# Two samples' counts stacked in one matmul and evicted as 16-bit integers

## The chip, the cores and the metric

The kernel runs on one core of a Trainium2 chip. A core has five engines that run side by side, each with its own instruction order: TensorE (matmuls; PE in the profile, and PEld for its weight loads), VectorE (DVE), ScalarE (ACT), GpSimd (POOL) and SyncE (SP, which here only issues DMAs). [...] The metric is device time in microseconds.

## The reference

A recommender's forward pass for 16384 samples: a mean of 32 word vectors of 300 floats, three means over 20 vectors of 64, four single vectors of 64, a "wide" sum of one float per lookup, and a small MLP.

```python
tok = word_emb[token_idx].mean(axis=1)               # 32 of 50000 rows, 300 wide
e1 = emb_mh1[mh1_idx].mean(axis=1)                   # 20 of 1000 rows, 64 wide
e2, e3 = ...                                         # 20 of 5000, 20 of 10000
o1, o2, o3, o4 = ...                                 # one row each of 100, 50, 20, 1000
emb = jnp.concatenate([tok, e1, e2, e3, o1, o2, o3, o4], axis=1)   # 748
wide = (the same lookups in tables of width 1, summed)[:, None]
h = jax.nn.relu(emb @ W1 + b1)                       # 1024
h = jax.nn.relu(h @ W2 + b2)                         # 512
h = jax.nn.relu(h @ W3 + b3)                         # 256
return jax.nn.sigmoid(h @ Wd + bd + wide)
```

## The kernel before, in words

The samples go through in 128 tiles of 128. Work is emitted in steps by one loop written out by hand (lines 570 to 620): 11 steps per tile (`STEPS`), 1408 steps with counts and 16 more to finish (`WAKE`), 1424 in all. Each engine executes its instructions in the order in which that loop emits them.

**Word vectors.** Each of the 128 x 32 sets of 128 rows is fetched by one indirect DMA that GpSimd issues (`tokens`, L255), two to a buffer, eight buffers (`TOK_BUFS`). `add_up` (L237 to L243) adds them into a PSUM accumulator on VectorE, three groups later (`TOK_LAG`). The loop hands out these gathers evenly over the 1424 steps.

**Small tables.** The seven small tables are not gathered. They lie on the chip as `terms`: 138 slices (`n_h`) of 128 rows, each row as three bf16 parts which together keep float precision (`convert_tables`). For each sample the kernel counts how often each table row is looked up, and multiplies the counts with the tables:

- `one_hots` (L322, VectorE) compares keys with an iota. For six samples of each half tile (`ONEHOT`; four in the last step of a tile) it makes `row1`, where lookup p hits row r of a slice, and `slice1`, where it hits slice h. A partition is one lookup: 64 lookups of a sample on partitions 0 to 63, 64 of another sample on 64 to 127. The one-hots for step i + 1 are emitted ahead of the counts of step i, in two buffers.
- `counts` (L340, TensorE) multiplies them: rows x slices, 128 x 138 counts for each sample. Each matmul uses 64 partitions, one sample's lookups; 12 in a full step.
- The eviction (L347, ScalarE) copies the 12 results out of PSUM as fp8 into `cnt`, ordered half, sample, slice.
- `small_sums` (L365, TensorE), for the tile before, takes for each slice the counts of its 128 samples as weights (`by_slice[:, :, h]`, elements 138 bytes apart) and `terms[:, h, :]` as the moving operand, and sums in PSUM over slices; VectorE adds the three parts up (L371).

**MLP.** Two tiles form a block. `Block.add_small` and `add_tokens` transpose the sums; `layer` (L461, TensorE, float32) makes the products, with a ReLU on ScalarE (L470) after each row of outputs, in two PSUM buffers `ph`. The loop spreads a block's layers over the steps (`Paced`). `early_part` (L443) begins the last block's first layer in the PSUM buffers of the counts.

Count results have one buffer `pc` of four PSUM banks. Indices are loaded by SyncE, `ix` for four tiles at a time (L276), and the keys brought into columns by a transpose (`key_columns`, L305).

Of the kernel before, what the change touches and what calls it, by code (L numbers as in the profile page):

```python
# [11 lines left out]
I32 = mybir.dt.int32  # L12
U32 = mybir.dt.uint32
AF = mybir.ActivationFunctionType
ALU = mybir.AluOpType
AX = mybir.AxisListType

P = 128
# [10 lines left out]
LAYER_TILES = 2  # L29
HALF = P // 2  # L30
N_SMALL = 3 * N_MH + 4
ONEHOT = 6
# [19 lines left out]
def kernel(  # L52
# [94 lines left out]
    terms = const.tile([P, n_h, 3 * ROW], BF16, name="terms")  # L147
    minus_half = const.tile([P, P], BF16, name="minus_half")
    nc.vector.tensor_single_scalar(minus_half, ident, -0.5, op=ALU.mult)

# [16 lines left out]
    def convert_tables():  # L167
# [19 lines left out]
        def make(p, c):  # L187

            if c == 0:
                nc.scalar.activation(term(p, 0), rows(p), AF.Copy, scale=2.0)  # L190
                return
            _, a, b = pieces[p]
            left = ps_h.tile([P, SPLIT, ROW], F32, name="left", tag="ph")[:, 0 : b - a, :]
            nc.tensor.matmul(left, ident, rows(p), start=True, stop=False)  # L194
            for k in range(c):
                nc.tensor.matmul(left, minus_half, term(p, k), start=False, stop=(k == c - 1))
            nc.scalar.activation(term(p, c), left, AF.Copy, scale=2.0)

# [67 lines left out]
    def load_indices(blk):  # L266


        b0 = blk * BLOCK
        it = idxp.tile([P, NSUB, N_TOK], I32, name="it")  # L270
        nc.sync.dma_start(
            out=it, in_=idx[b0 : b0 + BLOCK, 0:N_TOK].rearrange("(s p) c -> p s c", p=P)
        )
        ix = keyp.tile([P, NSUB // 2, 2, N_SMALL], I32, name="ix")
        for s in range(NSUB):
            nc.sync.dma_start(  # L276
                out=ix[(s % 2) * HALF : (s % 2 + 1) * HALF, s // 2],
                in_=idx[b0 + s * P : b0 + (s + 1) * P, IDX_MH:IDX_COLS].rearrange(
                    "(f p) c -> p f c", p=HALF
                ),  # L280
            )
        token_indices[blk] = it
        return ix
# [30 lines left out]
    def one_hots(sc, s, i):  # L314
# [5 lines left out]
        for w, (one, n) in enumerate(((row1, P), (slice1, n_h))):  # L320
            shape = [P, rows, n // 2, 2]
            nc.vector.tensor_tensor(  # L322
                one[:, 0:rows, :].rearrange("p i (n d) -> p i n d", d=2),
                iota[:, 0:n].rearrange("p (n d) -> p n d", d=2).unsqueeze(1).to_broadcast(shape),
                sc[:, s // 2, w, s % 2, b : b + rows, :].unsqueeze(2).to_broadcast(shape),
                ALU.is_equal,
            )
        return row1, slice1

    def counts(cnt, hot, i):  # L330
# [3 lines left out]
        n = rows // 2  # L334
        pc = ps_c.tile([P, 2, 2, 512], F32, name="pc")
        for k in range(rows):
            for f in range(2):
                half = slice(f * HALF, (f + 1) * HALF)
                at = k % n * n_h
                nc.tensor.matmul(  # L340
                    pc[:, f, k // n, at : at + n_h],
                    hot[0][half, k, :],
                    hot[1][half, k, :],
                    start=True,
                    stop=True,
                )
        nc.scalar.activation(  # L347
            cnt[:, :, b : b + rows, :].rearrange("l f (g k) h -> l f g (k h)", g=2),
            pc[:, :, :, 0 : n * n_h],
            AF.Copy,  # L350
            scale=0.5,
            saturate=False,
        )

    def small_sums(g, cnt):


        by_slice = cnt.rearrange("l f p h -> l (f p) h")
        for i in (0, 2, 4, 6):
            pair = SMALL[i : i + 2]  # L360
            pg = ps_g.tile([P, 2, 3 * ROW], F32, name="pg")
            for j, f in enumerate(pair):
                h0, h1 = slices[f]
                for h in range(h0, h1):
                    nc.tensor.matmul(  # L365
                        pg[:, j, :], by_slice[:, :, h], terms[:, h, :], start=(h == h0), stop=(h == h1 - 1)
                    )
# [69 lines left out]
    def early_part(block):  # L437


        part = ps_c.tile([P, 4, 512], F32, name="pc")  # L440
        for m in range(4):
            for k in range(NK - 3):
                nc.tensor.matmul(  # L443
                    part[:, m, 0 : block.n],
                    w1_sb[: chunk_k[k], k, m * P : (m + 1) * P],
                    block.chunk(k),
                    start=(k == 0),
                    stop=False,
                )
        return part  # L450

    def layer(dst, weights, bias, srcs, n_out, part=None):

        n = srcs[0].shape[-1]
        for m in range(n_out):
            begun = part is not None and m < 4
            ph = part[:, m, :] if begun else ps_h.tile([P, N], F32, name="ph", tag="ph")
            for k, src in enumerate(srcs):
# [111 lines left out]
    for step in range(n_steps):  # L570
        t, i = divmod(step, STEPS)
        s = t % NSUB
        if i == 0:
# [90 lines left out]
```

## Time and profile before

| | |
|---|---|
| median of 3 runs | 7548.09 us (7520.87 to 7551.03) |
| span of the profiled execution, first to last instruction | 5191.3 us |
| the profiled execution's own time beside its span | not given by the profile |
| TensorE busy, matmuls / weight loads | 5113.7 us (99%) / 4177.5 us (80%) |
| VectorE / ScalarE / GpSimd busy | 3890.9 (75%) / 2600.7 (50%) / 3888.4 us (75%) |
| mean granted TensorE clock | 0.998 |

A row of the costliest groups names a line, an engine, an operation, output <- input by the program's names, shapes and a count; after the bar stand the busy time in us and the mean of one in ns; after the second bar the idle time of the engine just before these instructions, and what ended most of it. A row of waits names who waited for whom: total us, times, longest. A row in order of time has start, duration, engine, line and how many instructions were merged. Matmuls overlap each other, so their pace is read from the spacing of starts.

### The profile page before, as it was taken

What the parts mean: (1) busy time and instruction counts of PE and PEld (TensorE: products, weight loads), DVE (VectorE), ACT (ScalarE), POOL (GpSimd) and SP (SyncE); (2) the same over time, 40 slices, a digit from 0 to 9 for tenths busy, and PEclk for the clock granted to TensorE, in tenths of its full rate; (3) what the DMA queues carried; (4) which work ended last, traced back from release to release, by engine and by line L of the source; (5) the groups of instructions that cost most, each with busy time, mean ns of one, the idle gap of its engine ahead of it and who ended that gap; (6) DMA issues with size and microseconds to landing.
All of it is one profiled execution on the core that took longest, in us unless ns stands there. A gap on an engine that the chain in (4) does not pass through costs nothing.

```text
span 5191.3 us, 116518 instructions
## 1 busy us (share of the span) xinstructions
PE 5113.7 (99%) x46912; PEld 4177.5 (80%) x46912; DVE 3890.9 (75%) x8502; ACT 2600.7 (50%) x2445; POOL 3888.4 (75%) x4103
## 2 busy tenths in 40 slices
PE   7999999999999999999999999999999999999999
PEld 5888888888888888888888888888888878888888
DVE  6777777777777777777777777777777777777773
ACT  6555555555545545545445455555555545555552
POOL 7777777777777777777777777777777777777774
PEclk9999999999999999999999999999999999999999
DMA  7444444444444444444444444444444444444442
GB/s 201 123 126 125 125 126 124 125 126 125 126 124 126 125 126 125 126 124 126 125 126 126 124 126 125 126 126 123 125 125 126 125 126 124 126 125 126 124 124 77
DMA packets 253019, 653.38 MB, mean 126 GB/s; under 512 B 119056, under 2 KB 119633, under 8 KB 252477
## 3 DMA queue, kind: packets, MB, share of 16 engines
q0 software_dynamic: 196608, 629.41, 44.2%
q1 hardware_dynamic: 55869, 16.53, 1.4%
q8 instruction: 367, 6.01, 0.5%
q14 instruction: 175, 1.43, 0.1%
HBM read 645.59 MB, written 0.07 MB: 124 GB/s over the span
## 4 chain that ended last, share of the span: by engine, by line
PE 94%; DVE 2%; issue 1%; DMA 1%; ACT 0%; POOL 0%; SPq 0%; DVEq 0%; ACTq 0%
PE ph L461 46%; PE pg L365 32%; PE pc L340 12%; PE po L486 1%; PE pt L426 1%; PE pt L410 1%; PE pt L407 1%; DMA tok_rows<-in_word_emb_dram,it 1%; DVE own L239 1%; DVE own L243 0%; DMA w_sb<-in_W_dram 0%; POOL tok_rows L255 0%; DVE slice L322 0%; PE left L194 0%; PE pt L427 0%
## 5 line engine op out<-in xcount | busy, mean ns | idle before, releaser
L255 POOL DMA_INDIRECT tok_rows<-in_word_emb_dram,it x4096 | 3887.5, 949 | 1260.5 <-issue 873.6
L347 ACT ACTIVATE cnt<-pc 128x1656 fp8e3<-128x1656 f32 (+1 forms) x1408 | 2124.6, 1509 | 1607.7 <-PE pc L340 1592.1
L365 PE MATMUL pg<-terms,cnt 128*128 128x195 bf16 x17664 | 1828.7, 253 | 7.9 <-DVE g L371 7.6
L365 PEld LDWEIGHTS <-cnt 128*128 128x128 fp8e3 x17664 | 1590.3, 144 | 162.1 <-issue 31.8
L461 PE MATMUL ph<-h,w_sb 128*128 128x256 f32 (+1 forms) x5200 | 1224.2, 379 | 0.5 <-ACT h L470 0.5
L461 PE MATMUL ph<-x_small,w_sb 128*128 128x256 f32 (+2 forms) x4128 | 1044.4, 381 | 4.8 <-DVE x_small L429 3.0
L461 PEld LDWEIGHTS ph<-h,w_sb 128*128 128x128 f32 x5200 | 930.8, 191 | 99.2 <-issue 0.8
L322 DVE TENSOR_TENSOR row<-own,sc 128x768 bf16<-128x768 bf16 (+1 forms) x1408 | 762.3, 541 | 304.2 <-PE pc L340 251.5
L239 DVE TENSOR_TENSOR own<-own,tok_rows 128x300 f32<-128x300 f32 x1920 | 917.0, 478 | 63.3
L243 DVE TENSOR_TENSOR own<-own,tok_rows 128x300 f32<-128x300 f32 x1792 | 856.8, 478 | 61.8
L340 PEld LDWEIGHTS <-row 64*128 64x128 bf16 x16384 | 495.4, 94 | 484.8 <-issue 227.5
L470 ACT ACTIVATE h<-ph,b_sb 128x256 f32<-128x256 f32 (+1 forms) x906 | 426.8, 471 | 912.3 <-PE ph L461 912.0
L461 PEld LDWEIGHTS ph<-x_small,w_sb 128*128 128x128 f32 (+1 forms) x4128 | 739.3, 191 | 86.6 <-PE ph L461 6.4
L322 DVE TENSOR_TENSOR slice<-own,sc 128x828 bf16<-128x828 bf16 (+1 forms) x1408 | 795.5, 565 | 0.0
L340 PE MATMUL pc<-slice,row 64*128 64x138 bf16 x16384 | 751.0, 223 | 15.8 <-DVE slice L322 9.0
L461 PE MATMUL ph<-x_tok,w_sb 128*128 128x256 f32 (+1 forms) x2064 | 565.4, 380 | 0.0
L371 DVE TENSOR_REDUCE g<-pg 128x130 f32<-128x390 f32 (+1 forms) x512 | 261.1, 510 | 393.6 <-PE pg L365 391.0
L461 PEld LDWEIGHTS ph<-x_tok,w_sb 128*128 128x128 f32 x2064 | 373.0, 192 | 40.9
L428 DVE TENSOR_SCALAR x_tok<-pt 128x256 f32<-128x256 f32 x128 | 54.4, 425 | 301.6 <-PE pt L427 301.6
L411 DVE TENSOR_TENSOR x_small<-pt,scale 128x384 f32<-128x384 f32 x128 | 71.2, 556 | 91.8 <-PE pt L410 91.8
L486 PE MATMUL po<-h,wd_sb 128*1 128x256 f32 (+1 forms) x260 | 68.0, 374 | 1.6 <-DVE x_small L429 1.0
L490 DVE TENSOR_TENSOR h<-po,wide_row 1x256 f32<-1x256 f32 (+1 forms) x65 | 26.5, 408 | 54.9 <-PE po L486 51.9
(55 smaller groups left out, 872.4 us busy)
## 6 DMA issues: line engine op xcount, KB each, us to landing
tok_rows<-in_word_emb_dram,it POOLq DMA_INDIRECT x4096
ix<-in_idx_dram SPq DMA_DIRECT2D x128, 32.0 KB
w_sb<-in_W_dram SPq DMA_DIRECT2D x6, 512.0 KB
raw<-in_mh_dram SPq DMA_DIRECT2D x4, 682.5 KB
it<-in_idx_dram SPq DMA_DIRECT2D x32, 64.0 KB
w_sb<-in_W_dram SPq DMA_DIRECT2D x1, 2048.0 KB
out_dram<-h SPq DMA_DIRECT2D x63, 1.0 KB
raw<-in_mh_dram SPq DMA_DIRECT2D x2, 227.5 KB
```

The source lines that it names most:

```text
L239: nc.vector.tensor_add(tok_sum, tok_sum, a)
L243: nc.vector.tensor_add(to, tok_sum, b)
L255: nc.gpsimd.indirect_dma_start(out=rows[:, r * TOK_D : (r + 1) * TOK_D], out_offset=None, in_=word, in_offset=bass.IndirectOffsetOnAxis(ap ...
L322: nc.vector.tensor_tensor(one[:, 0:rows, :].rearrange("p i (n d) -> p i n d", d=2), iota[:, 0:n].rearrange("p (n d) -> p n d", d=2).unsque ...
L340: nc.tensor.matmul(pc[:, f, k // n, at : at + n_h], hot[0][half, k, :], hot[1][half, k, :], start=True, stop=True,)
L347: nc.scalar.activation(cnt[:, :, b : b + rows, :].rearrange("l f (g k) h -> l f g (k h)", g=2), pc[:, :, :, 0 : n * n_h], AF.Copy, scale=0 ...
L365: nc.tensor.matmul(pg[:, j, :], by_slice[:, :, h], terms[:, h, :], start=(h == h0), stop=(h == h1 - 1))
L371: nc.vector.tensor_reduce(g[:, at : at + n * ROW].rearrange("p (f d) -> p f d", f=n), pg[:, 0:n, :].rearrange("p f (c d) -> p f d c", c=3) ...
L411: nc.vector.tensor_tensor(self.small[:, 0:3, at], pt[:, 0:3, :], scale.unsqueeze(2).to_broadcast([P, 3, P]), ALU.mult)
L461: nc.tensor.matmul(ph[:, 0:n], weights[: src.shape[0], k, m * P : (m + 1) * P], src, start=(k == 0), stop=(k == len(srcs) - 1),)
L470: nc.scalar.activation(dst[:, m, 0:n], ph[:, 0:n], AF.Relu, bias=bias[:, m : m + 1])
L486: nc.tensor.matmul(po[:, 0:n], wd_sb[:, k : k + 1], h3[:, k, 0:n], start=(k == 0), stop=(k == M3 - 1))
```

## The change

Two samples share one matmul. The one-hots of partitions 64 to 127 get the value 256 in place of 1 (a new ScalarE operation on `row1`), and one matmul over all 128 partitions yields count + 256 x count of the other sample. The eviction writes that as a 16-bit integer, whose two bytes are the two counts; `small_sums` reads the same bytes as fp8. Such a byte as fp8 is worth count/64, so `terms` are scaled by 64 where they were scaled by 2. `cnt` is ordered slice, sample, with the slice outermost, so the 128 weights of a slice are contiguous bytes; the two samples of a pair are now neighbours, and the index load says so. The counts get two PSUM buffers of two banks each, in which `early_part` takes two tiles for one.

```diff
+UPPER = 256.0
+COUNT = 64.0
-    ps_c = ctx.enter_context(tc.tile_pool(name="ps_c", bufs=1, space=bass.MemoryType.PSUM))
+    ps_c = ctx.enter_context(tc.tile_pool(name="ps_c", bufs=2, space=bass.MemoryType.PSUM))
...
-    nc.vector.tensor_single_scalar(minus_half, ident, -0.5, op=ALU.mult)
+    nc.vector.tensor_single_scalar(minus_count, ident, -1.0 / COUNT, op=ALU.mult)
...
-                nc.scalar.activation(term(p, 0), rows(p), AF.Copy, scale=2.0)
+                nc.scalar.activation(term(p, 0), rows(p), AF.Copy, scale=COUNT)
...
@@ load_indices
-                    "(f p) c -> p f c", p=HALF
+                    "(p f) c -> p f c", f=2
@@ one_hots, at its end
+        upper = row1[HALF:P, 0:rows, :]
+        nc.scalar.activation(upper, upper, AF.Copy, scale=UPPER)
         return row1, slice1
@@ counts
-        pc = ps_c.tile([P, 2, 2, 512], F32, name="pc")
+        pc = ps_c.tile([P, 2, 512], F32, name="pc")
         for k in range(rows):
-            for f in range(2):
-                half = slice(f * HALF, (f + 1) * HALF)
-                at = k % n * n_h
-                nc.tensor.matmul(
-                    pc[:, f, k // n, at : at + n_h],
-                    hot[0][half, k, :],
-                    hot[1][half, k, :],
-                    start=True,
-                    stop=True,
-                )
+            at = k % n * n_h
+            nc.tensor.matmul(
+                pc[:, k // n, at : at + n_h], hot[0][:, k, :], hot[1][:, k, :], start=True, stop=True
+            )
         nc.scalar.activation(
-            cnt[:, :, b : b + rows, :].rearrange("l f (g k) h -> l f g (k h)", g=2),
-            pc[:, :, :, 0 : n * n_h],
+            cnt[:, :, b : b + rows].rearrange("l h (g k) -> l h g k", g=2),
+            pc[:, :, 0 : n * n_h].rearrange("l g (k h) -> l h g k", h=n_h),
             AF.Copy,
-            scale=0.5,
-            saturate=False,
         )
@@ small_sums
-        by_slice = cnt.rearrange("l f p h -> l (f p) h")
+        by_slice = cnt.bitcast(FP8)
...
-                        pg[:, j, :], by_slice[:, :, h], terms[:, h, :], start=(h == h0), stop=(h == h1 - 1)
+                        pg[:, j, :], by_slice[:, h, :], terms[:, h, :], start=(h == h0), stop=(h == h1 - 1)
@@ early_part
-        part = ps_c.tile([P, 4, 512], F32, name="pc")
-        for m in range(4):
+        part = []
+        for pair in range(2):
+            two = ps_c.tile([P, 2, 512], F32, name="pc")
+            for m in range(2):
+                part.append(two[:, m, :])
...
@@ the loop
-                cnt = cp.tile([P, 2, HALF, n_h], FP8, name="cnt", tag="counts")
+                cnt = cp.tile([P, n_h, HALF], U16, name="cnt", tag="counts")
```

More of the change, by code (lines that the diff above doesn't have):

```diff
@@ L195, in make @@
             for k in range(c):
-                nc.tensor.matmul(left, minus_half, term(p, k), start=False, stop=(k == c - 1))
-            nc.scalar.activation(term(p, c), left, AF.Copy, scale=2.0)
+                nc.tensor.matmul(left, minus_count, term(p, k), start=False, stop=(k == c - 1))
+            nc.scalar.activation(term(p, c), left, AF.Copy, scale=COUNT)
         for step in range(len(pieces) + 2):
@@ L437, in early_part @@
     def early_part(block):
-        part = ps_c.tile([P, 4, 512], F32, name="pc")
-        for m in range(4):
[L442 to L449, printed above, removed]
+        part = []
[3 more added lines that the diff above has]
+                part.append(two[:, m, :])
+                for k in range(NK - 3):
+                    nc.tensor.matmul(
+                        part[-1][:, 0 : block.n],
+                        w1_sb[: chunk_k[k], k, (2 * pair + m) * P : (2 * pair + m + 1) * P],
+                        block.chunk(k),
+                        start=(k == 0),
+                        stop=False,
+                    )
         return part
@@ L456, in layer @@
             begun = part is not None and m < 4
[L457 removed]
+            ph = part[m] if begun else ps_h.tile([P, N], F32, name="ph", tag="ph")
             for k, src in enumerate(srcs):
```

3 lines of the change are left out of this document (2 added, 1 removed).

## The prediction

> **What bounds the kernel now.** I read the engines' busy shares first, then the costliest groups, then the stretches of the span, then who waits for whom.
>
> ```profile
> span 5191.3 us, 116518 instructions
> PE 5113.7 (99%) x46912; PEld 4177.5 (80%) x46912; DVE 3890.9 (75%) x8502; ACT 2600.7 (50%) x2445; POOL 3888.4 (75%) x4103
> PE 94%; DVE 2%; issue 1%; DMA 1%; ACT 0%; POOL 0%; SPq 0%; DVEq 0%; ACTq 0%
> L255 POOL DMA_INDIRECT tok_rows<-in_word_emb_dram,it x4096 | 3887.5, 949 | 1260.5 <-issue 873.6
> L347 ACT ACTIVATE cnt<-pc 128x1656 fp8e3<-128x1656 f32 (+1 forms) x1408 | 2124.6, 1509 | 1607.7 <-PE pc L340 1592.1
> L365 PE MATMUL pg<-terms,cnt 128*128 128x195 bf16 x17664 | 1828.7, 253 | 7.9 <-DVE g L371 7.6
> ```
>
> The first reading is that TensorE is the bound: busy 99%, and 94% of the chain that ended last. POOL looks idle a quarter of the time. It isn't. The row of L255 has 3887.5 us busy and 1260.5 us of idle time before its 4096 instructions: together 5148 of 5191 us. The idle part is 0.31 us for each one. The stretches of the span, with POOL's instructions alone, and the waits of POOL say whether that is waiting:
>
> ```profile
> 130.00:1300.00 1170.00, 885.60 (x934) 1.00 0.46 125
> 1300.00:2500.00 1200.00, 908.29 (x958) 1.00 0.46 125
> 2500.00:3800.00 1300.00, 983.91 (x1037) 1.00 0.46 125
> 3800.00:5080.00 1280.00, 969.04 (x1021) 1.00 0.46 125
> POOL tok_rows L255 <- issue: 873.6, 2866, 0.3
> POOL tok_rows L255 <- DVE own L239: 94.2, 309, 0.3
> POOL tok_rows L255 <- DVE own L243: 92.0, 267, 7.7
> L255 POOL DMA_INDIRECT tok_rows<-in_word_emb_dram,it x4096: 942/949/1323, 3.1 to 5148.6; - x196
> ```
>
> The columns of the first four rows are the stretch, its length, POOL's busy time and count, the granted TensorE clock, DMA share and GB/s. One gather starts every 1170/934 = 1.253, 1.253, 1.254 and 1.254 us: the same in every stretch. The longest single wait is 0.3 us whatever the name beside it (total over times is 0.30 everywhere), so those names are only what happened to end inside a fixed gap. One wait is real, 7.7 us near the end. So POOL issues its 4096 gathers without a pause from 3.1 to 5148.6 us. Two engines are at their limit at once: TensorE by its work, POOL by its issue rate. A change to one of them alone has the other to meet.
>
> [...] By the spans' 75% POOL would have room and the whole TensorE relief below would arrive (second rival); by the spacing almost none of it does.
>
> **The change part by part.**
>
> *Counts on TensorE.* Per full step 12 matmuls of 64 rows (all 12 within 0.54 us) become 6 of 128 rows. Their cost is read from the order of time on TensorE:
>
> ```profile
> 2502.50 0.59 PE L461 MATMUL ph<-h,w_sb 128*128 128x256 f32 x2
> 2503.03 0.54 PE L340 MATMUL pc<-slice,row 64*128 64x138 bf16 x12
> 2503.50 1.43 PE L365 MATMUL pg<-terms,cnt 128*128 128x195 bf16 x14
> 2504.77 1.92 PE L461 MATMUL ph<-h,w_sb 128*128 128x256 f32 x8
> 2506.62 0.55 PE L340 MATMUL pc<-slice,row 64*128 64x138 bf16 x12
> 3266.20 3.05 PE ph L461 x14
> 2384.42 2.73 DMA tok_rows<-in_word_emb_dram,it
> 249.64 0.40 PE L305 MATMUL pk<-ident_bf,keys 128*128 128x128 bf16 x4 [1.14 <-DVE wide_row L415]
> 249.88 0.52 PE L365 MATMUL pg<-terms,cnt 128*128 128x195 bf16 x4
> L340 PEld LDWEIGHTS <-row 64*128 64x128 bf16 x16384 | 495.4, 94 | 484.8 <-issue 227.5
> ```
>
> A layer matmul takes 3.05/14 = 0.218 us in a row of its own kind. The two at 2502.50 start 0.21 apart (0.59 minus the 0.38 of one), the second near 2502.72; the count after it starts at 2503.03, 0.31 later: 0.095 us lost at the border. The loads ahead of the counts show the same stop: 484.8 us idle over 1408 steps, 0.34 each, for nothing that they wait for. From the first count to the first sum there is 0.47 us. So a step's counts cost about 0.565 us. The nearest row with full 128x128 bf16 weights is the key transpose: four take 249.88 - 249.64 = 0.24 us, 0.060 each for 128 columns; with 138 columns I take 0.063, so six cost 0.38 us and no border, as their neighbours use 128 rows too. Saving 0.185 us x 1408 = 260 us. Bounds: if the border stays, 0.095 x 1408 = 134 less; if loads were to hide better, some 30 more.
>
> [...]
>
> *Sums on TensorE.* The 17664 matmuls of L365 stay; their weights `by_slice[:, h, :]` become contiguous bytes where they were 138 bytes apart. Now 14 take 2504.77 - 2503.50 = 1.27 us, 0.091 each. At the transposes' pace per column (0.060 x 195/128 = 0.091) that is the matmul itself, and the gain is nothing. If instead the load sets the pace (144 ns each against the transposes' 98, rows below), 0.091 shrinks by 98/144 to 0.062: 0.029 x 17664 = 510 us. I take a seventh, 0.004 each or 70 us, near the lower end since the pace per column fits so well.
>
> ```profile
> L365 PEld LDWEIGHTS <-cnt 128*128 128x128 fp8e3 x17664 | 1590.3, 144 | 162.1 <-issue 31.8
> L305 PEld LDWEIGHTS <-keys 128*128 128x128 bf16 x128 | 7.5, 98 | 47.3 <-DVE wide_row L415 38.5 <-DVE keys L294 6.4 <-DVE x_small L429 2.1
> L347 ACT ACTIVATE cnt<-pc 128x1656 fp8e3<-128x1656 f32 x1280 | 1985.4, 1551 | 1512.6 <-PE pc L340 1497.0 <-issue 11.8 <-PE pg L365 2.4
> L347 ACT ACTIVATE cnt<-pc 128x1104 fp8e3<-128x1104 f32 x128 | 139.3, 1088 | 95.1 <-PE pc L340 95.1
> L470 ACT ACTIVATE h<-ph,b_sb 128x256 f32<-128x256 f32 (+1 forms) x906 | 426.8, 471 | 912.3 <-PE ph L461 912.0
> DVE row L322 <- PE pc L340: 251.5, 270, 3.1
> PE pc L340 <- ACT cnt L347: 6.8, 7, 1.6
> ```
>
> *ACT.* The eviction shrinks from 1656 to 828 elements. Two sizes give (1551 - 1088)/552 = 0.839 ns an element, so 828 take 0.856 us. New is the scaling of `upper`, 768 elements on 64 partitions: 1.551 - 888 x 0.839 = 0.81 us. Sum 1.66 for 1.55 us: ACT goes from 50% to some 53%, off the path, since it waits 1592 us for the counts already. Cost 0, and no gain, because nobody waits for the eviction; the bound from above is the third rival.
>
> *The new wait.* `upper` waits for DVE's `row`, the counts wait for `upper`, and behind `upper` on ACT stand this step's eviction and ReLUs, for which TensorE's layers wait. What hides it: DVE makes one-hots a step ahead, stopped 270 times because counts still hold the buffer. A step is 5191/1424 = 3.6 us, 0.81 fits in it. Without that cover it would be 0.81 us a step, 1140 us. I take 0.
>
> *Two count buffers* take away 6.8 us of waits. The stacked index load, the scale 64 and the two-tile `early_part` issue as many DMAs, DVE operations and matmuls as before: 0. No queue is passed by a moved step.
>
> *Sum.* TensorE's work falls by 260 + 70 = 330 us, to 4784, 3.36 us a step. POOL needs 4096 x 1.254 = 5136 us, 3.61 a step, and nothing of it changes. So TensorE will stop at the token sums: DVE's additions will wait for gathers to land, the next `row` behind them, and the counts for that. What is left to gain is the time in which TensorE held POOL up, and the tail:
>
> ```profile
> L239 DVE TENSOR_TENSOR own<-own,tok_rows x1920: 453/478/479, 14.6 to 5161.8; 128x300 f32<-128x300 f32 x192
> 5187.63 0.91 PE L486 MATMUL po<-h,wd_sb 128*1 128x128 f32 x4
> ```
>
> Before, the last gather starts at 5148.6 and could at best start at 3.1 + 4095 x 1.254 = 5138 (7.4 of the 10 is the one long wait). The last addition starts at 5161.8, 13 us after the last gather, where a landing takes 2.7 us, as the chain's piece at 2384.42 shows; the last layers then need the same 29 us. So the end could come earlier by 7 us (the wait alone) up to 10 + 7 = 17 us (the lateness too, less the lag of three groups). I take the middle, 12: span 5179 us. Nothing excludes 0, if the layer work of the last 90 us is the limit by itself.
>
> *Own time.* The profile gives the execution only its span, 5191.3 us; the median of the runs is 7548.1, 2356.8 more. What lies there no row shows. I keep it as it is: 7548 - 12 = **7536 us**. If it grew with the span, 7531: no difference that counts.
>
> **The rivals.**
>
> 1. *Forecast: POOL's issue rate is the floor.* For: a spacing equal to 0.001 us in four stretches. 7536; own range 7515 to 7555 (0 to 17 us, and the runs' own spread of 7521 to 7551).
> 2. *The floor isn't there in the timed runs.* For: they take 2357 us more than the profiled span, and if part of that is TensorE running slower, or if gathers issue faster there, TensorE is the bound alone. Then the 330 us arrive in full: 7548 - 330 - 12 = 7206, or part of it; each 0.01 us off the spacing gives 41 us. Against: nothing shows two kinds of execution.
> 3. *Slower: the 16-bit eviction.* It writes runs of six elements, 12 bytes, 128 bytes apart, and reads with a stride. It decides once it takes more than POOL's 3.61 a step less 0.81 for `upper` and 0.30 of ReLUs (426.8/1424): 2.5 us, 2.9 times my 0.856. At 3.1 us (twice today's) a step is 4.21 us: 1408 x 4.21 + 93 (from the last eviction, 5098.0, to the end) = 6021, time 8378. Against, on the reading side: rows below, where 390 strided elements of PSUM (L371) cost DVE what 384 contiguous ones (L411) do. [...] No run here shows such a write.
> 4. *The change doesn't do what it says:* the border stays and sums gain nothing. TensorE still has 126 us of relief or so, POOL is the floor as before: 7540, no change either.
>
> ```profile
> L347 ACT ACTIVATE cnt<-pc x1408: 1082/1551/1553, 10.5 to 5098.0; 128x1656 fp8e3<-128x1656 f32 x160, 128x1104 fp8e3<-128x1104 f32 x16
> L371 DVE TENSOR_REDUCE g<-pg 128x130 f32<-128x390 f32 x384 | 215.6, 561 | 374.9 <-PE pg L365 373.4
> L411 DVE TENSOR_TENSOR x_small<-pt,scale 128x384 f32<-128x384 f32 x128 | 71.2, 556 | 91.8 <-PE pt L410 91.8
> ```
>
> **How the numbers follow.** A change under 0.5% (38 us) can't be told from none here. Forecast 0.68, second 0.23, third 0.05, fourth 0.04. Faster 0.23, same 0.72, slower 0.05. The second case spreads from 7206 to 7510; a lower end of 7380 takes in about 0.4 of it, an upper end of 7570 all but the third: left out are 0.14 + 0.05.
>
> **What would show it.** Right: L255's starts stay 1.254 us apart, TensorE's busy time falls by some 330 us and its new idle time ends at DVE or at gathers' landings; the additions L239 wait for tok_rows; counts start 0.22 us after the layer matmul before them; ACT's eviction takes 0.86 us and `upper` 0.81. Wrong: gathers closer together, or a time that falls by more than 40 us with the spacing unchanged; an eviction over 2.5 us; TensorE waiting for ACT at the counts.

## The result and the profile after

| | before | changed |
|---|---|---|
| median of the runs beside each other | 7548.3 us (7520.9 to 7551.0) | 7210.0 us (7192.3 to 7216.5) |
| span / granted clock of the profiled execution | 5191.3 us / 0.998 | 7190.5 us / 0.871 |
| TensorE, matmuls | 5113.7 us, 46912 | 5640.4 us, 38720 |
| ScalarE | 2600.7 us | 2838.5 us |

The ratio is 0.9554 (0.9534 to 0.9573): 338 us are gone, where 12 were forecast. The second rival's price was 7206.

The profile after is of another kind than the one before. First its page: span, busy times, the granted clock in 40 slices, and the chain that ended last.

```profile
span 7190.5 us, 102784 instructions
PE 5640.4 (78%) x38720; PEld 4635.0 (64%) x38720; DVE 3881.9 (54%) x8502; ACT 2838.5 (39%) x3853; POOL 3876.3 (54%) x4103
...
PEclk8888888888898888888888888888888888888888
...
PE 61%; issue 14%; another core or an unknown queue 12%; DVE 8%; ACT 4%; DVEq 0%; SPq 0%; DMA 0%; ACTq 0%
```

The span is within 2 us of that execution's time (7192.3), so nothing of size lies outside a span. TensorE has fewer matmuls and yet more busy time than before, at a clock of 0.871. Next three of the costliest groups of the changed kernel. In such rows "remote", like "another core or an unknown queue" in the chain above, is a wait for whose end the profile finds no event:

```profile
L258 POOL DMA_INDIRECT tok_rows<-in_word_emb_dram,it x4096 | 3875.4, 946 | 3270.9 <-DVE own L246 1982.1 <-issue 884.7 <-DVE own L242 122.9
...
L346 ACT ACTIVATE cnt<-pc 128x828 uint16<-128x828 f32 x1280 | 1108.7, 866 | 1559.1 <-remote 792.7 <-PE pc L343 478.2 <-PE ph L461 134.8
L332 ACT ACTIVATE row<-row 64x768 bf16<-64x768 bf16 x1280 | 1075.0, 840 | 571.3 <-DVE row L325 473.4 <-issue 39.3 <-DVE keys L298 21.7
```

its waits:

```profile
POOL tok_rows L258 <- DVE own L246: 1982.1, 573, 17.2
...
PEld L362 <- issue: 885.4, 985, 7.0
...
PE pg L362 <- issue: 614.0, 815, 6.1
...
PEld L343 <- ACT row L332: 112.9, 89, 5.1
```

and two of the stretches, with POOL's instructions alone:

```profile
130.00:1300.00 1170.00, 635.37 (x673) 0.85 0.34 90
...
3800.00:5080.00 1280.00, 708.05 (x749) 0.88 0.34 92
```

POOL starts a gather every 1170/673 = 1.74 us, not 1.25, and really waits: 1982 us for additions (longest wait 17 us, where before every wait but one was 0.3). So the gathers are not the floor in this execution. TensorE stands still as well: its loads at L362 for 885 us, its matmuls there for 614 us, put down to "issue", which is to say to nothing that the profile can name. That label is weaker evidence here than in the profile before, because this trace holds only 6076 of the 8018 updates of VectorE's semaphore (from whose records the profile tells who waited for VectorE), where the trace before holds 7710 of 7738. In order of time, TensorE alone, such a stop looks like this:

```profile
407.24 0.62 PE L461 MATMUL ph<-x_small,w_sb 108*128 108x256 f32 x2
407.91 0.38 PE L461 MATMUL ph<-x_tok,w_sb 128*128 128x256 f32 x1
409.44 0.38 PE L461 MATMUL ph<-x_tok,w_sb 128*128 128x256 f32 x1 [1.15 <-issue]
410.92 0.38 PE L461 MATMUL ph<-x_tok,w_sb 128*128 128x256 f32 x1 [1.11 <-issue]
412.32 0.38 PE L461 MATMUL ph<-x_tok,w_sb 128*128 128x256 f32 x1 [1.02 <-issue]
413.02 1.49 PE L461 MATMUL ph<-x_small,w_sb 128*128 128x256 f32 x2 [0.33 <-issue]
414.31 0.90 PE L343 MATMUL pc<-slice,row 128*128 128x138 bf16 x6
415.00 1.35 PE L362 MATMUL pg<-terms,cnt 128*128 128x195 bf16 x7
```

From 407.91 on four layer matmuls start 1.40 to 1.53 us apart, with no wait that the profile names (elsewhere they start 0.218 apart). After them six counts take 0.69 us, from 414.31 to 415.00, where they take 0.37 in an execution without stops (below). The granted clock of that piece is in its stretches, with TensorE's matmuls alone (stretch, length, busy time and count, clock, DMA share, GB/s):

```profile
408.00:412.90 4.90, 1.41 (x4) 1.00 0.61 152
412.95:416.30 3.35, 3.16 (x16) 0.50 0.17 46
```

The clock is full during the stop and half behind it (1.00 and 0.50). The whole trace has 272 stretches at half clock, 1861 of 7190 us together, which gives the mean of 0.871; the trace before, which has few such gaps (below), has 4, with 22 us.

Over the whole trace, weight loads and matmuls together, 1583 starts follow the one before by more than 0.62 us, and these gaps hold 1829 us. In the profile of before there are 71, with 85 us. Of the 1583, 1188 with 931 us stand before an instruction that waits for no semaphore at all (before: 3, with 2 us); there TensorE stops without waiting. The other 395, with 897 us, stand at a wait, and how much of these is only the lateness that a stop leaves behind isn't shown.

### The profile page after: what moved, and what is told of

It is laid out like the page before. It is cut to its first block, busy times and chain, and to the rows that moved or that the text cites. A ratio compares the mean times of both kernels' runs of the same rounds, so it can differ in the third digit from the quotient of the medians.

```text
span 7190.5 us, 102784 instructions
## 1 busy us (share of the span) xinstructions
PE 5640.4 (78%) x38720; PEld 4635.0 (64%) x38720; DVE 3881.9 (54%) x8502; ACT 2838.5 (39%) x3853; POOL 3876.3 (54%) x4103
## 3 DMA queue, kind: packets, MB, share of 16 engines
q0 software_dynamic: 196608, 629.41, 32.5%
## 4 chain that ended last, share of the span: by engine, by line
PE 61%; issue 14%; another core or an unknown queue 12%; DVE 8%; ACT 4%; DVEq 0%; SPq 0%; DMA 0%; ACTq 0%
PE ph L461 30%; PE pg L362 21%; PE pc L343 7%; DVE own L246 2%; DVE own L242 2%; ACT row L332 2%; ACT cnt L346 2%; DVE row L325 1%; DVE slice L325 1%; ACT h L470 1%; PE po L486 1%; PE pt L407 1%; DVE g L368 0%; PE pt L423 0%
## 5 line engine op out<-in xcount | busy, mean ns | idle before, releaser
L362 PE MATMUL pg<-terms,cnt 128*128 128x195 bf16 x17664 | 2103.8, 266 | 753.4 <-issue 614.0
L362 PEld LDWEIGHTS <-cnt 128*128 128x128 fp8e3 x17664 | 1656.8, 105 | 927.1 <-issue 885.4
L346 ACT ACTIVATE cnt<-pc 128x828 uint16<-128x828 f32 (+1 forms) x1408 | 1189.3, 845 | 1613.5 <-remote 806.1
L461 PE MATMUL ph<-h,w_sb 128*128 128x256 f32 (+1 forms) x5200 | 1392.8, 413 | 94.4 <-issue 60.0
L332 ACT ACTIVATE row<-row 64x768 bf16<-64x768 bf16 (+1 forms) x1408 | 1155.2, 820 | 675.4 <-DVE row L325 550.2
L461 PE MATMUL ph<-x_small,w_sb 128*128 128x256 f32 (+2 forms) x4128 | 1172.9, 412 | 91.0 <-issue 60.5
L461 PEld LDWEIGHTS ph<-h,w_sb 128*128 128x128 f32 x5200 | 1021.5, 209 | 295.1 <-issue 126.9
L343 PE MATMUL pc<-slice,row 128*128 128x138 bf16 x8192 | 809.3, 233 | 215.6 <-issue 130.9
L343 PEld LDWEIGHTS <-row 128*128 128x128 bf16 x8192 | 641.8, 103 | 512.6 <-issue 210.0
L461 PEld LDWEIGHTS ph<-x_small,w_sb 128*128 128x128 f32 (+1 forms) x4128 | 810.3, 210 | 234.0 <-issue 98.7
L461 PE MATMUL ph<-x_tok,w_sb 128*128 128x256 f32 (+1 forms) x2064 | 636.4, 417 | 13.3 <-issue 12.7
## 6 DMA issues: line engine op xcount, KB each, us to landing
raw<-in_mh_dram SPq DMA_DIRECT2D x2, 227.5 KB
```

Of the source, the lines that this page charges most:

```text
L332: nc.scalar.activation(upper, upper, AF.Copy, scale=UPPER)
L343: nc.tensor.matmul(pc[:, k // n, at : at + n_h], hot[0][:, k, :], hot[1][:, k, :], start=True, stop=True)
L346: nc.scalar.activation(cnt[:, :, b : b + rows].rearrange("l h (g k) -> l h g k", g=2), pc[:, :, 0 : n * n_h].rearrange("l g (k h) -> l h g ...
L362: nc.tensor.matmul(pg[:, j, :], by_slice[:, h, :], terms[:, h, :], start=(h == h0), stop=(h == h1 - 1))
L461: nc.tensor.matmul(ph[:, 0:n], weights[: src.shape[0], k, m * P : (m + 1) * P], src, start=(k == 0), stop=(k == len(srcs) - 1),)
```

## The experiments

The question was first whether the 338 us come from time that the profile shown doesn't hold (TensorE alone is the bound in the timed executions) or from a POOL floor lower than forecast; then what the stops hang on; then what the parts of the change are worth.

All times are in one table; each row's kernel was timed beside the kernel before on the same chip. e1 to e5 are five sessions, each on a chip of its own. "Before" is the median of the kernel before there.

| run | before, us | this, us | ratio (95%) | granted clock |
|---|---|---|---|---|
| e1_before_again | 7669.8 | 7670.9 | 0.9998 (0.9984 to 1.0013) | 0.875 |
| e1_few_gathers | 7669.8 | 4845.9 | 0.6311 (0.6296 to 0.6326) | 0.998 |
| e1_one_buffer | 7669.8 | 7406.1 | 0.9643 (0.9619 to 0.9668) | 0.862 |
| e1_contig_only | 7669.8 | 7653.7 | 0.9970 (0.9950 to 0.9989) | 0.873 |
| e2_before_few_gathers | 5193.5 | 5193.8 | 0.9999 (0.9988 to 1.0010) | 0.997 |
| e2_half_gathers | 5193.5 | 4834.2 | 0.9308 (0.9281 to 0.9335) | 0.998 |
| e2_plain_loads | 5193.5 | 4834.6 | 0.9308 (0.9281 to 0.9335) | 0.998 |
| e2_quarter_rows | 5193.5 | 5168.5 | 0.9950 (0.9928 to 0.9973) | 0.992 |
| e3_after_again | 7659.6 | 7314.5 | 0.9551 (0.9535 to 0.9567) | 0.867 |
| e3_quarter_rows | 7659.6 | 7215.1 | 0.9421 (0.9372 to 0.9469) | 0.874 |
| e3_plain_loads | 7659.6 | 4836.7 | 0.6315 (0.6302 to 0.6328) | 0.998 |
| e3_no_upper | 7659.6 | 7260.3 | 0.9480 (0.9464 to 0.9496) | 0.870 |
| e4_after_third | 5193.9 | 5166.3 | 0.9947 (0.9927 to 0.9967) | 0.993 |
| e4_half_gathers | 5193.9 | 4831.2 | 0.9302 (0.9283 to 0.9320) | 0.999 |
| e4_bufs_4 | 5193.9 | 5181.0 | 0.9974 (0.9965 to 0.9984) | 0.990 |
| e4_bufs_5 | 5193.9 | 5175.6 | 0.9965 (0.9951 to 0.9979) | 0.993 |
| e5_bufs_4 | 7648.6 | 7302.7 | 0.9532 (0.9491 to 0.9572) | 0.866 |
| e5_half_gathers | 7648.6 | 4855.6 | 0.6346 (0.6316 to 0.6376) | 0.998 |

The column "before" holds the main finding. The same kernel takes 5193.5 and 5193.9 us on two chips and 7648.6, 7659.6 and 7669.8 us on three others, in every one of its runs there (lowest and highest lie within 60 us). These are called the lower and the upper level below. As each chip was used in one session, it isn't shown whether the level belongs to the chip or to the session. The runs that the prediction had, 7548, are near the upper level; the profile beside them, with a span of 5191.3, is one of the lower.

### Is the time inside the span? The kernel before, unchanged

No edit.

> The kernel before, unchanged, to be profiled beside the others. Theory F (TensorE's instruction stream stops for a few us in every 256 or so instructions, for nothing that it waits for, and these stops fill the 2357 us between the first profile and the timed runs): span about 7546 us as in the timed runs, granted clock below 0.9 as after the change (0.871), and some 1900 to 2300 us of gaps on TensorE put down to 'issue'. Theory P (gathers on POOL are the floor, and what lies around the span is fixed): span 5191 us again, clock 0.998, gathers 1.254 us apart, time 7548.

Its profiled execution has a span of 7681.5 us. Its page, and then its waits:

```profile
span 7681.5 us, 116518 instructions
PE 6018.2 (78%) x46912; PEld 4707.8 (61%) x46912; DVE 3890.4 (51%) x8502; ACT 2576.7 (34%) x2445; POOL 3878.4 (50%) x4103
...
PEclk8888888888888888888888899898888988888889
```

```profile
POOL tok_rows L255 <- DVE own L243: 2465.6, 677, 16.6
...
PEld L340 <- issue: 1208.0, 1324, 14.1
...
PEld L365 <- issue: 592.4, 896, 6.6
```

The kernel before has the same stops at this level (1358 gaps of over 0.62 us on TensorE, 1827 us), and POOL has slack in it. What was taken for "own time" is inside the span.

One part of theory F isn't borne out: the stops are not tied to every 256 instructions. In the trace after, the gaps lie all over blocks of 256, with 71 to 134 us in each sixteenth of a block. This speaks against late loading of code, too: the trace after has 306 packets of 16 KB on the queue for instructions (q8), one for every 253 of TensorE's 77440 loads and matmuls. They took a median of 1.00 us each, and 0.97 us in the trace of e4_after_third, which has no such stops.

### Take the gathers away, at both levels

```diff
-                rows = tokp.tile([P, TOK_GROUP * TOK_D], F32, name="tok_rows")
-                for r in range(TOK_GROUP):
+                if q % 8 == 0:                                   # half_gathers: q % 2
+                    rows = tokp.tile([P, TOK_GROUP * TOK_D], F32, name="tok_rows")
+                for r in range(TOK_GROUP if q % 8 == 0 else 0):  # half_gathers: q % 2
```

The edit is made in the changed kernel, and for e2_before_few_gathers in the kernel before.

> The changed kernel with an eighth of the gathers: two of a tile's 32 gathers in every half tile are made, and VectorE adds the same rows again, so the word sums are not the reference's. Theory P (POOL's pace or a landing is waited for): with POOL out of the way the time falls by hundreds of us. Theory F with stops that gathers cause: below 5300 us, TensorE's issue gaps gone, clock near 1. Theory F with stops of TensorE's own: 7150 to 7210 us, gaps as after the change.

> The kernel before with an eighth of the gathers, as the changed kernel was run at 4846 us (word sums are not the reference's): the two without the stops. Theory A (TensorE's work and the stops add up, and the change only cuts the work): 5190 us, so that the difference to 4846 is the same 340 us as with all gathers (7548 - 7210); a counts step still loses 0.19 us at its borders. Theory B (the gain comes from fewer stops, as TensorE issues 16384 instructions fewer): the difference is much smaller than 340, below 5000 us.

> The changed kernel with half of the gathers (every second group adds the rows of the one before; word sums not the reference's). If each gather costs TensorE its share (some 2480/4096 = 0.6 us): 4846 + 0.6 x 1536 = 5770 to 6090 us. If the stops come only when gathers crowd: 4850 to 5000 us. If a few gathers are enough to bring all stops: 7000 us.

> Half of the gathers, as run before at the lower level, where it took 4834 us (word sums not the reference's). At the upper level: if every gather costs TensorE the same 0.6 us, 4835 + 1240 = 6075 us; if only long unbroken runs do, 4835 to 5000 us, since POOL then has pauses anyway.

> Half of the gathers, which took 4831 us at the lower level (word sums not the reference's). At the upper level: 6075 us if every gather costs TensorE the same 0.6 us, 4835 to 5000 us if only long unbroken runs do.

The page of the changed kernel with an eighth of the gathers, and page and waits of the one with half of them, both where the kernel before is at the upper level:

```profile
span 4844.6 us, 93826 instructions
PE 4752.5 (98%) x38720; PEld 4225.0 (87%) x38720; DVE 3880.5 (80%) x8502; ACT 2842.3 (59%) x3853; POOL 491.6 (10%) x519
```

```profile
span 4850.7 us, 97666 instructions
PE 4752.5 (98%) x38720; PEld 4222.5 (87%) x38720; DVE 3881.1 (80%) x8502; ACT 2842.2 (59%) x3853; POOL 1946.9 (40%) x2055
```

```profile
POOL tok_rows L259 <- DVE own L246: 2133.3, 828, 10.0
```

Without its full number of gathers the changed kernel takes 4831 to 4856 us on every chip, TensorE busy 98% at a clock of 0.998: there is no upper level any more. That is its TensorE work. For the kernel before the same bound is 5193.8, measured at the lower level alone. The change cuts TensorE's work by 5193.8 - 4845.9 = **348 us**, as exact as the spread of 4831 to 4856 allows; 330 had been forecast. Half the gathers remove the stops wholly. A fixed price of 0.6 us a gather (2466/4096, see below) would have left half of the stops and given some 6075 us: that idea falls with 4855.6.

### Same rows' bytes without POOL; same POOL work with a quarter of the bytes

```diff
# plain_loads
-                    nc.gpsimd.indirect_dma_start(...)
+                    row0 = (t * N_TOK + j) % (word.shape[0] // P) * P
+                    nc.sync.dma_start(out=rows[:, r * TOK_D : (r + 1) * TOK_D], in_=word[row0 : row0 + P, :])
# quarter_rows: pieces of 300 bytes, in 8 zeroed buffers used in turn
-                        out=rows[:, r * TOK_D : (r + 1) * TOK_D],
+                        out=rows[:, r * TOK_D : r * TOK_D + TOK_D // 4],
-                        in_=word,
+                        in_=word.rearrange("v (c d) -> (v c) d", d=TOK_D // 4),
```

> The changed kernel with the 4096 gathers replaced by as many plain loads of 128 consecutive rows, issued by SyncE; bytes and buffers as before, POOL idle (word sums not the reference's). If the stops come from gathers issued by POOL: 4850 to 4900 us, no stops. If they come from that many bytes moving into SBUF: 7200 to 7330 us.

> The changed kernel with all 4096 gathers, each row 300 bytes instead of 1200 (the rest of a row is zeros; word sums not the reference's). If the stops come from the bytes that the gathers move: 4850 to 5300 us, limited by POOL's 1.254 us a gather (5180). If they come from issuing gathers or from their number of packets: 7200 to 7330 us, stops as after the change.

> 4096 plain loads issued by SyncE in place of the gathers, as run before, where it took 4835 us beside a kernel before at 5193 (word sums not the reference's). If the kernel before is at the lower level again: 4835. If it is at the upper level: 4835 where the stops need gathers by POOL or scattered rows, 7200 or so where that many bytes into SBUF are enough.

> All 4096 gathers with rows of 300 bytes, as run before, where it took 5168 us beside a kernel before at 5193 (word sums not the reference's). If the kernel before is at the lower level again: 5168. If it is at the upper level: 5170 where the stops need the gathers' bytes, 7200 to 7330 where issuing them is enough.

Lower level first. Plain loads of the same bytes give 4834.6: TensorE's bound. A quarter of the bytes in as many gathers gives 5168.5, 2 us from the changed kernel on the other chip of that level. So there the floor is the number of gathers that POOL issues, not the bytes. Upper level: plain loads give 4836.7 and no stops; a quarter of the bytes gives 7215.1 (two runs, 7183 and 7247), all the stops but some 100 us of the changed kernel's on that chip (7314.5). The pages with a row of the DMA queues, of e3_plain_loads and e3_quarter_rows:

```profile
span 4834.1 us, 102462 instructions
PE 4752.0 (98%) x38720; PEld 4225.0 (87%) x38720; DVE 3877.7 (80%) x8502; ACT 2840.5 (59%) x3853; POOL 0.9 (0%) x7
...
q1 hardware_dynamic: 645693, 645.93, 47.0%
```

```profile
span 7245.1 us, 104709 instructions
PE 5701.0 (79%) x38720; PEld 4678.1 (65%) x38720; DVE 3887.8 (54%) x8510; ACT 2838.6 (39%) x3853; POOL 3867.7 (53%) x4103
...
q0 software_dynamic: 131072, 157.55, 13.4%
```

646 MB by SyncE's DMAs keep the DMA engines 47% busy and disturb TensorE not at all; 158 MB by POOL's gathers, 13%, come with nearly all of the stops. The bytes are little of the cause; the gathers that POOL issues are needed for it. Two limits remain. The plain loads differ from the gathers both in who issues them and in that their rows are consecutive, and no run tells these apart. And quarter_rows, as its edit reads, doesn't fetch a quarter of each row: index i picks the i-th piece of 300 bytes, so all pieces lie in the first quarter of the table.

### The changed kernel at each level

No edit.

> The changed kernel, unchanged, beside the kernel before once more. Runs of the kernel before so far lie at two levels, 7548 to 7670 us and 5193 us. At the lower level, theory P: POOL's issue is the floor, 5168 to 5180 us (the run with quarter rows, same 4096 gathers, had 5168), 0.3 to 0.5% below the kernel before, DVE waiting for gathers to land. At the upper level, theory A: 340 us below the kernel before, TensorE's gaps as before.

> The changed kernel beside the next three. If the kernel before stands at 5193 here: 5165 to 5185 us, at POOL's floor. If it stands at 7550 to 7670: 0.955 of that.

At the upper level the ratio repeats, 0.9551 (0.9535 to 0.9567). At the lower the same change gains 28 us, 0.9947 (0.9927 to 0.9967). Page, stretches with POOL's instructions alone, and waits of that execution:

```profile
span 5163.6 us, 102784 instructions
PE 4826.0 (93%) x38720; PEld 4244.1 (82%) x38720; DVE 3849.3 (75%) x8502; ACT 2842.6 (55%) x3853; POOL 3875.1 (75%) x4103
...
DMA 29%; issue 19%; DVE 19%; PE 19%; POOL 13%; ACT 2%; DVEq 0%; SPq 0%; POOLq 0%; ACTq 0%
```

```profile
130.00:1300.00 1170.00, 884.97 (x936) 0.99 0.46 125
...
3800.00:5080.00 1280.00, 968.40 (x1024) 0.99 0.46 125
```

```profile
DVE own L246 <- DMA tok_rows<-in_word_emb_dram,it: 473.5, 774, 2.8
...
DVE own L242 <- DMA tok_rows<-in_word_emb_dram,it: 241.1, 341, 3.0
```

This is the forecast's picture at this level: gathers 1.250 us apart in both stretches, the additions now wait 715 us for landings, TensorE is down to 93%, and the chain has gone over to DMA, VectorE and POOL.

### The parts of the change

```diff
# one_buffer, in the changed kernel (and a first layer begun in one tile, not two)
-    ps_c = ctx.enter_context(tc.tile_pool(name="ps_c", bufs=2, ...))
+    ps_c = ctx.enter_context(tc.tile_pool(name="ps_c", bufs=1, ...))
# no_upper, in the changed kernel
-        upper = row1[HALF:P, 0:rows, :]
-        nc.scalar.activation(upper, upper, AF.Copy, scale=UPPER)
# contig_only, in the kernel before: fp8 counts, slices outermost
-            cnt[:, :, b : b + rows, :].rearrange("l f (g k) h -> l f g (k h)", g=2),
-            pc[:, :, :, 0 : n * n_h],
+            cnt[:, :, :, b : b + rows].rearrange("l h f (g k) -> l h f g k", g=2),
+            pc[:, :, :, 0 : n * n_h].rearrange("l f g (k h) -> l h f g k", h=n_h),
...
-        by_slice = cnt.rearrange("l f p h -> l (f p) h")
+        by_slice = cnt.rearrange("l h f p -> l h (f p)")
...
-                        pg[:, j, :], by_slice[:, :, h], terms[:, h, :], start=(h == h0), stop=(h == h1 - 1)
+                        pg[:, j, :], by_slice[:, h, :], terms[:, h, :], start=(h == h0), stop=(h == h1 - 1)
...
-                cnt = cp.tile([P, 2, HALF, n_h], FP8, name="cnt", tag="counts")
+                cnt = cp.tile([P, n_h, 2, HALF], FP8, name="cnt", tag="counts")
```

> One part undone: the changed kernel with one count buffer instead of two (the last block's early part then covers two of its row groups, not four). Theory F and theory W: 7210 us, nothing (before, only 6.8 us of waits stood there). Rival: with stops on TensorE the eviction is late more often, and the second buffer carries part of the gain: 7250 to 7350 us.

> One part alone: the kernel before with counts ordered slice, half, sample, so that the sums' weights are contiguous bytes; matmuls of 64 rows, fp8 eviction and one buffer stay. TensorE issues as many instructions as before. Theory F: stops as before, only the sums' own 0.091 us shrinks a little: 7450 to 7548 us. Theory W (the gain of 338 us is the shorter work of the matmuls, by their spacing): 70 to 140 us of it come from here, 7410 to 7480 us.

> The changed kernel without the scaling by 256 on ScalarE (both samples' counts then add up, so the small sums are not the reference's): the new wait DVE row, ACT upper, TensorE counts is gone. At the lower level: no difference to the changed kernel (its cover of a step holds). At the upper level: the changed kernel's profile has TensorE waiting 180 us for ACT's row (112.9 and 66.6), so up to 180 us faster; if another wait takes its place, 0 to 50.

The first two forecasts are in us from the first session's 7548, and the chip of e1 is slower (7670); so the ratios decide.

*One buffer.* 0.9643 against the changed kernel's 0.9554 and 0.9551, which were measured on other chips: the second buffer is worth 0.9% of 7670, some 70 us, at the upper level (by the ends of the intervals, 35 to 103). The rival was right that it carries part of the gain. The row of waits says why the 6.8 us read from the lower level's profile was no measure of it:

```profile
PE pc L343 <- ACT cnt L346: 675.6, 294, 7.8
```

In the changed kernel, with two buffers, the same wait has 0.9 us. The likely reason is that after a stop everything is late at once, and a single buffer makes TensorE wait for the eviction before it may go on.

*Contiguous counts alone* gain 0.3%, 8 to 38 us by the interval. That lies within theory F's gain of 0 to 98 us and below theory W's 70 to 140. The loads are shorter, as in the changed kernel, but the eviction, which now writes runs of six bytes, grew from 1549 ns (e1_before_again) to 1619 ns, 90 us over 1280 of them, and TensorE's wait for it (`PE pc` for `ACT cnt`) grew from 349 to 427 us. That this wait ate up the gain is likely, but no run shows it alone. Groups of e1_contig_only:

```profile
L347 ACT ACTIVATE cnt<-pc 128x1656 fp8e3<-128x1656 f32 x1280 | 2072.9, 1619 | 3029.7 <-remote 1587.5 <-PE pc L340 896.2 <-PE ph L461 330.6
L365 PEld LDWEIGHTS <-cnt 128*128 128x128 fp8e3 x17664 | 1641.9, 106 | 722.2 <-issue 567.5
```

*Without the scaling* the changed kernel takes 7260.3 where it takes 7314.5 on that chip: 54 us. By the ends of the intervals it is 30 to 79 us. The scaling and its wait, costed at 0, are worth that much at the upper level.

### Do unbroken runs of gathers matter? Fewer word buffers

In the trace after, TensorE's slow starts (0.62 to 0.78 us apart) lie mostly behind the later gathers of an unbroken run (gathers up to 1.4 us apart). That width takes in 1081 of the 1583 gaps: 911 of them behind the 1100 gathers that come seventh to twelfth in theirs, 119 behind the 2569 that come first to fifth. With half the gathers a run has two of them on average. This alone doesn't say what comes first: a stop makes VectorE late, which makes POOL wait, so a stop can also be what ends the run. Fewer buffers were meant to cut the runs.

```diff
-TOK_BUFS = 8
+TOK_BUFS = 4        # bufs_5: 5
```

> The changed kernel with four buffers for gathered rows instead of eight, so that POOL waits for VectorE every two gathers once four groups are under way; all gathers stay. Theory R (runs): at the upper level the stops go, and the time falls to 5200 to 5700 us, bound by the alternation of gather, landing and addition. Theory N (number): 7300 us or more, as every gather stays. At the lower level both say 5180 to 5400.

> As with four buffers, but five: up to ten gathers can stand in a row. Theory R: between the run with four and the changed kernel with eight, 5300 to 6800 us at the upper level; theory N: 7300 us. At the lower level 5170 to 5250.

> Four buffers for gathered rows instead of eight, which took 5181 us at the lower level. At the upper level, theory R (unbroken runs of gathers bring the stops): 5200 to 5700 us; theory N (every gather has its share): 7300 us or 0.955 of the kernel before.

At the lower level they are 15 and 9 us slower than eight buffers (5181.0 and 5175.6 against 5166.3). At the upper level the stops stay, 7302.7 and clock 0.866. It decides nothing about the idea: POOL's runs were hardly shorter, 6.5 gathers on average against 6.7, so the edit didn't change what it was to change. An unbroken run alone is not enough in any case, since at the lower level POOL issues without a pause and TensorE doesn't stop. No version tried that still computes the whole result is clearly faster than the changed kernel.

## Why the prediction was wrong

**The step that failed is "Own time".** It put 2356.8 us beside the span, called them fixed, and read the bound from a profile of 5191.3 us. Those microseconds lie inside the spans of the timed runs, as stops and slow clock on TensorE; the profile shown was of an execution without them. The second rival said that POOL's floor isn't there in the timed runs, and was given 0.23; it thought of a slower TensorE or faster gathers, not of stops. Its "against: nothing shows two kinds of execution" was the misreading: span and median 45% apart, with no row for the difference, were the sign.

**Why TensorE's relief arrives in full at the upper level.** There the time is TensorE's work and a nearly fixed amount of stops. Over the bounds without stops (5193.8 and 4845.9) the first runs stand 2354 us before and 2364 after; on the chip of e3_after_again, 2466 and 2469. POOL, with 1982 us of waits, has room to follow. 348 us of work come out as 338 and 345 us of time. Why the stops keep their amount isn't shown.

**What was luck.** The second rival's 7206 lies 4 us from the measured 7210, but its terms don't hold so closely. It took 330 us of work where 348 went, added 12 us that belong to POOL's floor, and left out the second buffer (about +70 us of gain) and the scaling (about -54).

**What was right.** POOL's floor is real at the level of the profile from which it was read: 28 us gained there (17 to 38 by the interval), forecast 12 and at most 17. The kernel before was not held by POOL, though: with an eighth of the gathers it takes the same 5193.8 us, so TensorE alone bounds it there. What the sum had wrong there is the spacing, which it held fixed at 1.254 us:

```profile
L258 POOL DMA_INDIRECT tok_rows<-in_word_emb_dram,it x4096: 940/946/1195, 3.0 to 5125.6; - x196
```

In e4_after_third the last gather starts at 5125.6 us, 23 us earlier than before. The median spacing is 1.251 us, 12 us less over 4095 gathers, and fewer starts come late, the other 11. Behind the last gather 38.0 us are left, where there were 42.7. Whether the 3 ns belong to the change or to the chip isn't shown. That the prediction took the spacing of POOL's starts in place of their spans is borne out there: spans of 0.946 us stand 1.250 apart, and 300-byte rows leave the floor where it is (5168.5 us beside 5166.3).

**The terms of the sum.** Read from order of time on TensorE in two executions without stops, the kernel before with an eighth of its gathers and then the changed kernel with an eighth:

```profile
2502.73 1.92 PE L462 MATMUL ph<-h,w_sb 128*128 128x256 f32 x8
2504.58 0.54 PE L341 MATMUL pc<-slice,row 64*128 64x138 bf16 x12
2505.05 1.43 PE L366 MATMUL pg<-terms,cnt 128*128 128x195 bf16 x14
2506.32 1.92 PE L462 MATMUL ph<-h,w_sb 128*128 128x256 f32 x8
```

```profile
2499.45 2.11 PE L462 MATMUL ph<-h,w_sb 128*128 128x256 f32 x9
2501.39 0.53 PE L344 MATMUL pc<-slice,row 128*128 128x138 bf16 x6
2501.76 1.54 PE L363 MATMUL pg<-terms,cnt 128*128 128x195 bf16 x16
2503.14 1.05 PE L462 MATMUL ph<-h,w_sb 128*128 128x256 f32 x4
```

- *Border.* The rows bear out 0.095 us at the entrance of the counts. Nine layer matmuls to the first count take 1.94 us, 0.216 each: no border is left. Before, eight take 1.85, 0.11 more than eight at 0.218. Over all steps the median from the last layer matmul to the first count is 0.312 before and 0.216 after. The fourth rival (the border stays) is out. That the border goes when the counts use 128 rows like their neighbours was the author's estimate: these rows show that it is gone, none shows what it was. The prediction's second witness for the border was misread: of the 484.8 us of idle time ahead of the loads its own row puts only 227.5 down to "issue", so they are not all "for nothing that they wait for".
- *Counts.* 0.47 us become 0.37 (forecast 0.38). With the border 0.096 + 0.10 = 0.196 a step, 1408 of them 276 us; forecast 260.
- *Sums.* 1.27/14 = 0.0907 became 1.38/16 = 0.0863 each; 17664 of them 78 us; forecast 70. 276 + 78 = 354, beside the 348 measured.
- *ACT.* Eviction 866 ns (forecast 856), scaling 840 (810), ScalarE 2838 us. The third rival needed 2.5 us and is out: writing runs of 12 bytes of two-byte elements, the eviction took 10 ns more than the two-size slope gave.
- *Two buffers, new wait.* Costed at 6.8 and 0 us; about 70 and 54 at the upper level, of opposite sign. The 6.8 was read from an execution without stops.

**What stays open.** What sets the level: each of five chips had one level through its whole session. One trait goes with it. With half the gathers the trace holds 21261 of 36864 updates of the semaphores that tell of landings at the upper level (e5_half_gathers), where TensorE doesn't stop, and 35827 at the lower (e4_half_gathers); with all gathers it is 21934 of 69632 (changed kernel, upper) and 68219 (e4_after_third). With plain loads nearly all are there at both. So at the upper level these records go missing already where no time is lost. Whether that has to do with the stops isn't shown, nor whether TensorE also stops in an execution that isn't recorded.

What in the gathers stops TensorE is open as well. It takes POOL's gathers at their full number, not their bytes, and half of them do nothing; whether it is their rate, their number of packets (196608, with 300-byte pieces 131072, with half the gathers 98304), their unbroken runs, their scattered rows, or something that goes along with these wasn't separated.

## What to carry to other kernels

Hold the span of a profile against the time that is to be predicted before any other reading; if they are far apart, the profile is of another execution, and each engine that it calls the bound must be asked about again in the one that is timed. Take a resource that is near its limit away in a kernel of its own (half the gathers, plain loads): that gives the next bound as a measured number, 4846 us here, and shows whether a floor holds. The worth of a buffer or a wait depends on how regular the flow is: 6.8 us of waits in an even execution came to about 70 us in one with stops.

## What the hardware showed that was not expected

- One kernel had two levels of time, one for each chip and session: 5194 and 7649 to 7670 us, granted clock 0.997 and 0.875.
- At the upper level TensorE stops, in good part (931 of 1829 us of gaps) with nothing to wait for. With the slow clock's share this costs 2354 to 2477 us, only beside 4096 gathers issued by POOL; 2048 gathers, or the same 629 MB by SyncE from consecutive rows, give none (4856 and 4837 us).
- Records go missing at that level: 6076 of 8018 updates of VectorE's semaphore are in the trace, 8004 at the lower level. A wait put down to "issue" or "remote" in such a trace is weak evidence.
- A gather of 128 rows costs POOL 1.25 us at the lower level whether it fetches 1200 or 300 bytes a row: starts 1.250 us apart in e4_after_third; 5127.8 us of busy and idle time for 4096 gathers, 1.252 each, in e2_quarter_rows (5166 and 5169 us in all).
- Going from 128-row layer matmuls to 64-row counts cost 0.096 us a step; the way back wasn't priced. Weights 138 bytes apart load in 144 ns, contiguous ones in 98 to 106, of which only 4 ns a matmul reach the end.
